# An LSTM of 512 steps on one core: h Wh in 512 columns and one PSUM bank, instead of 384 and 128 columns in two

## The chip, the cores and the metric

The kernel runs on one core of a Trainium2 chip. The metric is the device time of one execution in microseconds (us), lower is better. It is the median of three runs; the trace comes from one further, profiled execution.

## The reference

For 32 sequences (batch B = 32) of T = 512 steps with 512 features, an LSTM with 512 hidden units is run from a given first state, and its outputs are added to the input. Everything is float32.

```python
xW = jnp.einsum('ntd,dg->ntg', x, Wx) + b
def step(carry, xw_t):
    prev_h, prev_c = carry
    a = xw_t + prev_h @ Wh
    i = jax.nn.sigmoid(a[:, :Hd])
    f = jax.nn.sigmoid(a[:, Hd:2 * Hd])
    o = jax.nn.sigmoid(a[:, 2 * Hd:3 * Hd])
    g = jnp.tanh(a[:, 3 * Hd:])
    next_c = f * prev_c + i * g
    next_h = o * jnp.tanh(next_c)
    return ((next_h, next_c), next_h)
...
x = x + hs
```

The part x Wx does not depend on earlier steps. The part h Wh (prev_h @ Wh) and the cell behind it do, so they form a chain through all 512 steps.

## The kernel before

**Layout.** The hidden units are cut into four blocks of 128. A bank of PSUM, `gates[i]` (128 partitions x 512 float32), holds the four gates of one step: partitions 32j to 32j+31 hold the 32 sequences for unit block j, and the 512 columns are the gates i, f, g, o, each with 128 units (`IFG = 3 * P` = 384 is where o begins). There are two such banks. The state h is kept transposed in `ht` (128 x 4 x 32): block k holds units 128k to 128k+127 on the partitions and the 32 sequences in its columns.

**h Wh** (`h_part`, L1051). One matmul has `ht[:, k, :]` as its stationary operand (32 columns) and columns of block (k, j) of Wh as its moving operand; it adds into 32 partitions of a bank. Four matmuls, j = 0 to 3, write four different groups of 32 partitions; below they are called a group. Each float32 matmul is two instructions in the trace, so that one k is two groups. Before the change the gates i, f, g (384 columns) are done for all k first, in the bank `gates[t % 2]`, then o (128 columns) for all k, in the other bank, `gates[(t + 1) % 2]`.

**x Wx** is worked out during the same steps, some 16 steps ahead, by a scheme with fewer multiplications: a block of 8 x 4 rows takes 26 jobs in 32 steps, and a job has seven x products of 256 columns that `IN_STEPS` (L312) spreads over five steps. Such an x product is eight matmul instructions (two groups). After h Wh of a step TensorE therefore has five, six or (early) seven x products to do (`products`, L717). VectorE and ScalarE combine them (`evacuate`, L733: lines 768 to 787, 896, 908, 924), DMAs store the results in DRAM, and further DMAs on the POOL queue add them to a row that ScalarE has filled with the bias (`fill_bias`, L995, `load_xw`, L999).

**The cell** (`cell`, L1082). ScalarE takes sigmoid of i and f (L1092), tanh of g (L1093), sigmoid of o (L1094); VectorE makes f c, i g and their sum c (L1095 to 1097); ScalarE takes tanh of c (L1098); VectorE multiplies by o (L1099) and transposes blocks of 32 x 32 into the next `ht` (L1100). POOL adds the residual (L1162). Then ScalarE puts x Wx of later steps into the banks, as the value to which h Wh is added: `seed_first(k + 2)` the 384 columns of i, f, g (L1040), `seed_last(k + 1)` the 128 of o (L1046).

**Order.** All engines take their instructions in the order of the program text (`manual_schedule`). In step k the main loop (L1410) issues: h Wh of step k; the combining of x products; the x products of this step; loads; the cell of step k; the seeds. So TensorE does h Wh, then x products while ScalarE and VectorE do the cell, then h Wh of the next step, which needs the new `ht`. Semaphores between engines are set by the framework from what the instructions read and write.

**The end.** From step `HALVES` = 472 on, `h_halves` (L1064) and `cell_halves` (L1104) do the cell in two halves of 64 units per block. There the work on the first half is cut further, into pieces of 32 columns (L1132, L1134).

Of the kernel before, what the change touches and what calls it, by code (L numbers as in the profile page):

```python
# [10 lines left out]
AF = mybir.ActivationFunctionType  # L11
# [3 lines left out]
P = 128  # L15
B = 32
T = 512
NJ = 4
G = 4
IFG = 3 * P  # L20
# [145 lines left out]
PAIR_AT = len(UNITS)  # L166
PAIRS = len(PAIR_A_OF)
SECOND_AT = PAIR_AT + PAIRS
OFF = 16
# [22 lines left out]
HALVES = LAST + 3 - OFF  # L192
# [38 lines left out]
LATE_AT = [LAST + 2 + SPACING * u for u in range(NJ + 2)]  # L231
# [6 lines left out]
)  # L238
FILL_FROM, FILL_TO = LAST + 4, T - 4 + OFF
AT_LAST = 3  # L240


class Scheme:
# [68 lines left out]
IN_STEPS = ((4, (4,)), (2, (7,)), (0, (1,)), (1, (6,)), (0, (5,)), (1, (5,)), (3, (2, 3)))  # L312
# [7 lines left out]
def kernel(  # L320
# [9 lines left out]
    nc = tc.nc  # L330
# [11 lines left out]
    gates = [psum.tile([P, G * P], F32, name=f"gates_{i}") for i in range(2)]  # L342
# [14 lines left out]
    rows, xw, stored = {}, {}, {}  # L357
# [109 lines left out]
    late, stored_sums, sums_made = [], set(), []  # L467
# [211 lines left out]
    jobs = {}  # L679
# [283 lines left out]
    pieces = [(t, q, e) for t in range(LATE_END, T - 1) for q in range(NJ) for e in (slice(0, C), slice(C, 2 * C))]  # L963
# [11 lines left out]
    def tail_products(v):  # L975
# [5 lines left out]
        whole.clear()  # L981
        goal = given[1] + (total - 2 * AT_LAST - given[1]) * (v - FILL_FROM) // (FILL_TO - FILL_FROM)
        goal = min(goal, total - 2 * AT_LAST + AT_LAST * max(0, v - FILL_TO))
        while pieces and given[0] < goal:
# [23 lines left out]
    def half(a, m):  # L1008

        return a.rearrange("p (g u) -> p g u", u=P)[:, :, m * HP : (m + 1) * HP]  # L1010

    def bank_half(m, t=0):

        bank = halves[m] if t < T - 1 else jobs[LATE_AT[0]].pp[m].rearrange("p n c -> p (n c)")
        return bank[:, 0 : G * HP].rearrange("p (g u) -> p g u", u=HP)
# [16 lines left out]
    def seed_half(t, m):  # L1032
        if t < T - 1:
            nc.scalar.copy(bank_half(m), half(xw[t], m))

    def seed_first(t):
        if t == HALVES:
            seed_half(t, 0)
        elif t < HALVES:
            nc.scalar.copy(gates[t % 2][:, 0:IFG], xw[t][:, 0:IFG])  # L1040

    def seed_last(t):
        if t == HALVES:
            seed_half(t, 1)
        elif t < HALVES:
            nc.scalar.copy(gates[(t + 1) % 2][:, IFG:], xw[t][:, IFG:])  # L1046

    state.update(c=c_init, ht=h_init)
    ig = work.tile([P, P], F32, name="ig")

    def h_part(t):  # L1051
        for g, cols in ((gates[t % 2], slice(0, IFG)), (gates[(t + 1) % 2], slice(IFG, G * P))):
            for k in range(NJ):
                for j in range(NJ):
                    nc.tensor.matmul(  # L1055
                        g[j * B : (j + 1) * B, cols],
                        state["ht"][:, k, :],
                        wh_sb[:, k, j, cols],
                        start=False,
                        stop=True,  # L1060
                        skip_group_check=True,
                    )
# [19 lines left out]
    def cell(t):  # L1082
        n, tt = divmod(t, ROW)
        s = work.tile([P, G, P], F32, name=f"s_{t}", tag="s")
        fc = work.tile([P, P], F32, name=f"fc_{t}", tag="fc")
        c = work.tile([P, P], F32, name=f"c_{t}", tag="c", bufs=2)
        tc_t, h = ig, fc
        ht = work.tile([P, NJ, B], F32, name=f"ht_{t}", tag="ht", bufs=3)

        g = gates[t % 2].rearrange("p (g u) -> p g u", u=P)  # L1090
        o = gates[(t + 1) % 2].rearrange("p (g u) -> p g u", u=P)[:, 3]
        nc.scalar.activation(s[:, 0:2], g[:, 0:2], AF.Sigmoid)  # L1092
        nc.scalar.activation(s[:, 2], g[:, 2], AF.Tanh)  # L1093
        nc.scalar.activation(s[:, 3], o, AF.Sigmoid)  # L1094
        nc.vector.tensor_mul(fc, s[:, 1], state["c"])  # L1095
        nc.vector.tensor_mul(ig, s[:, 0], s[:, 2])
        nc.vector.tensor_add(c, fc, ig)  # L1097
        nc.scalar.activation(tc_t, c, AF.Tanh)  # L1098
        nc.vector.tensor_mul(h, s[:, 3], tc_t)  # L1099
        nc.vector.transpose(ht.rearrange("p q b -> p (q b)"), h)  # L1100
        state["c"], state["ht"] = c, ht
        put_step(t)

# [68 lines left out]
    for u, (i, j) in zip(UNIT_AT, UNITS):  # L1172
        job = new_job(u)
        job.kind = (i, j)
    for run in RUNS:
        for n in range(run.scheme.r):
            job = new_job(run.at + run.scheme.begin(n), run.scheme.late5(n))
            job.kind = (run, n)
    for w, j in zip(LATE_AT, LATE_ORDER):
        job = new_job(w, True)  # L1180
# [158 lines left out]
    with tc.manual_schedule():  # L1339
        warm = work.tile([P, G, P], F32, name="warm", tag="s")  # L1340
        nc.scalar.activation(warm[:, 0], c_init, AF.Sigmoid)
        zeros = c_init.bitcast(mybir.dt.bfloat16)
        for m in range(16):
            z, times = (zeros, 2) if m < 2 * NJ else (c_init, 4)
            nc.tensor.matmul(
                pps[m // NJ if m < 2 * NJ else 2][m % NJ * B : (m % NJ + 1) * B].rearrange("p n c -> p (n c)"),
                z[:, 0:B],
                z.unsqueeze(1).to_broadcast([P, times, z.shape[1]]),
                start=True,
                stop=True,  # L1350
            )
        made = [prepare(v) for v in range(EARLY)]
        first, second = jobs[0], jobs[1]
        parts = [t_sums(i) for i in (0, NJ)]
        for k in range(2):
            product(first, 1, k)
            product(first, 2, k)
        copy_first(first)
        for op in parts[0]:
            op()  # L1360
        made[0].pop(0)()
        parts[1].pop(0)()
        made[0].pop(0)()
        parts[1].pop(0)()
        product(first, 5)
        copy_fifth(first)
        product(first, 6)
        made[0].pop()()
        product(first, 3)
        product(second, 1)  # L1370
        copy_first(second)
        product(second, 2)
        nc.vector.tensor_add(first.pu[:, 1], first.acc, first.p5)
        parts[1].pop()()
        made[0].pop()()
        for op in (*made[1][:2], made[1][3], made[1][2]):
            op()
        product(second, 5)
        copy_fifth(second)
        product(second, 6)  # L1380
        product(second, 3)
        more = [op for j in range(1, NJ) for op in t_pair(j)]
        more.pop(0)()
        nc.vector.tensor_add(second.pu[:, 1], second.acc, second.p5)
        for v in range(EARLY, OFF):
            head(v)
            if v == NJ + 2:
                nc.vector.transpose(
                    bias_sb.rearrange("p (m l) -> p m l", l=B),
                    bias_t.unsqueeze(2).to_broadcast([P, G * NJ, B]),  # L1390
                )
            if XW_AT <= v + 1 < XW_AT + 4:
                fill_bias(v + 1 - XW_AT)
            announce(v)
            if XW_AT <= v < XW_AT + 3:
                load_xw(v - XW_AT)
            run_due(v + 1, 0)
            evacuate_at_first(v)
            for op in prepare(v):
                op()  # L1400
            for op in more[: NJ + EARLY - v - (v == EARLY)]:
                more.pop(0)()
            run_due(v + 1, (FILL_ROOM if v >= 4 else FILL_ROOM // 2) if v < PAIR_AT else 0)
            products(v)
            fetch(v)
        seed_first(0)
        seed_last(0)
        seed_first(1)

        for k in range(T):  # L1410
            if k % 2 == 0 and k + 2 < T:
                load_residual(k + 2)
            (h_part if k < HALVES else h_halves)(k)
            v = k + OFF
            if v < START + 14:
                head(v)
            announce(v)
            for op in prepare(v):
                op()
            room = HEAD_ROOM if v < START - 4 else ROOM if k < HALVES - 1 else HALF_ROOM  # L1420
            lacks = 0
            if v < START + 8:
                lacks = sum(len(ss) for late, ss in IN_STEPS if v - late not in jobs and (late, ss) != (1, (5,)))
                room -= FEWER * lacks
            run_due(v, room - evacuate(v, room))
            products(v)
            tail_products(v)
            if k + 3 < LATE_END:
                load_xw(k + 3)
            store_sums()  # L1430
            fetch(v)
            if k == T - 2:
                x_last()
            if k + 4 < LATE_END and lacks < 2:
                fill_bias(k + 4)
            (cell if k < HALVES else cell_halves)(k)
            if k + 4 < LATE_END and lacks >= 2:
                fill_bias(k + 4)
            seed_first(k + 2)
            seed_last(k + 1)  # L1440
        assert not due


# [49 lines left out]
```

## Time and profile before

| | |
|---|---|
| median of 3 runs | 3069.54 us (3068.2 to 3071.56) |
| profiled execution, first to last instruction (span) | 3067.7 us; no other time of this execution is given |
| granted TensorE clock | 1.000 |
| VectorE busy | 2322.4 us (76%) |
| ScalarE busy | 2001.6 us (65%) |
| POOL busy | 832.4 us (27%) |

In the rows below, PE is TensorE's matmuls, PEld its weight loads, DVE VectorE, ACT ScalarE. A row of the timeline has the start and the duration in us, the engine, the line, the operation, the tile written and the tiles read, the shapes, the count of instructions that were merged, and in brackets the idle time of the engine before it and what ended it. A row of groups has the busy time in us and the mean duration in ns behind the first bar, and the idle time before the group behind the second. The ends of matmuls are modelled, so starts are used.

### The profile page before, as it was taken

The page shows a single profiled execution, that of the slowest core. Times are in us where ns is not written, and L with a number is a line of the kernel's source. Part 1 is how long each engine was busy: PE and PEld are TensorE (multiplying, and loading weights), DVE is VectorE, ACT ScalarE, POOL GpSimd, SP SyncE. Part 2 cuts the span into 40 slices and gives each one's busy share as a digit, 9 for nine tenths or more (in the row PEclk, how much of TensorE's full clock was granted, in tenths as well). Part 3 has the DMA queues.
Part 4 walks back from the last instruction along what each step waited for, and adds up shares of the span by engine and source line. Part 5 has one row for each costly group of instructions (what it writes and reads, how often), then busy time and mean ns, then how long its engine had stood idle before and what let it go on. Part 6 is the DMA issues. An engine that isn't in the chain of part 4 may idle for free.

```text
span 3067.7 us, 133937 instructions
## 1 busy us (share of the span) xinstructions
PE 3059.4 (100%) x56568; PEld 2303.0 (75%) x56568; DVE 2322.4 (76%) x6622; ACT 2001.6 (65%) x5774; POOL 832.4 (27%) x1041
## 2 busy tenths in 40 slices
PE   9999999999999999999999999999999999999999
PEld 5566666667777777777777777777777777777766
DVE  7888777777777777777777777777777777777754
ACT  4666666666666666666666666766666666666665
POOL 0233222222222222222222222222222222222331
PEclk9999999999999999999999999999999999999999
DMA  9999898988889888898888988889898898888763
GB/s 330 291 272 266 230 253 213 255 232 234 245 212 260 227 237 246 215 262 215 257 227 214 271 218 244 233 222 261 216 253 232 222 259 222 250 233 220 199 120 72
DMA packets 345192, 716.21 MB, mean 233 GB/s; under 512 B 45712, under 2 KB 112016, under 8 KB 344080
## 3 DMA queue, kind: packets, MB, share of 16 engines
q1 hardware_dynamic: 268768, 564.74, 56.0%
q0 software_dynamic: 75392, 142.38, 27.9%
q8 instruction: 445, 7.29, 1.0%
q14 instruction: 155, 1.27, 0.1%
q10 hardware_dynamic: 432, 0.53, 0.1%
HBM read 521.48 MB, written 185.99 MB: 231 GB/s over the span
## 4 chain that ended last, share of the span: by engine, by line
PE 99%; DVE 0%; ACT 0%; DMA 0%; issue 0%; SPq 0%; ACTq 0%; DVEq 0%
PE gates L1055 52%; PE pp L708 18%; PE acc L708 18%; PE p L708 6%; PE gates L1069 4%; PE acc L950 0%; DMA raw_sb<-in_L_cond_Wx_dram 0%; PE pp L1069 0%; PE pp L950 0%; PE gates L708 0%; PE pp L1023 0%; DVE fc L1132 0%; ACT s L1114 0%; DVE ht L1134 0%; DVE c L1122 0%
## 5 line engine op out<-in xcount | busy, mean ns | idle before, releaser
L1055 PE MATMUL gates<-wh_sb,ht 128*32 128x384 f32 (+1 forms) x30144 | 1771.8, 379 | 0.4 <-ACT tt_sb L896 0.3
L1055 PEld LDWEIGHTS gates<-wh_sb,ht 128*32 128x32 f32 x30144 | 1318.1, 110 | 431.7 <-issue 131.1
L1162 POOL TENSOR_TENSOR oc<-xr,ht 128x128 f32<-128x128 f32 x509 | 389.2, 765 | 2108.0 <-DVE ht L1100 1919.5
L1001 POOL DMA_DIRECT2D xw<-xw x508 | 446.7, 879 | 93.3 <-DVE s L667 62.2
L1092 ACT ACTIVATE s<-gates 128x256 f32<-128x256 f32 x472 | 181.2, 384 | 350.5 <-PE gates L1055 340.2
L708 PE MATMUL pp<-wb,nodes 128*32 128x256 f32 x4000 | 370.9, 379 | 0.0
L997 ACT COPY xw<-bias_sb 128x512 f32<-128x512 f32 x508 | 320.9, 632 | 0.0
L776 ACT COPY pp<-pu 128x512 f32<-128x512 f32 x404 | 243.4, 602 | 57.4 <-DVE raw_sb L908 23.9
L1099 DVE TENSOR_TENSOR fc<-s,ig 128x128 f32<-128x128 f32 x472 | 137.9, 292 | 177.4 <-ACT ig L1098 177.4
L1095 DVE TENSOR_TENSOR fc<-s,c 128x128 f32<-128x128 f32 x471 | 136.7, 290 | 169.0 <-ACT s L1092 165.8
L708 PE MATMUL pp<-wb,s 128*32 128x256 f32 x2704 | 250.4, 379 | 0.0
L708 PE MATMUL acc<-wb,s 128*32 128x256 f32 x2704 | 250.3, 379 | 0.0
L708 PE MATMUL acc<-wa,s 128*32 128x256 f32 x2704 | 250.1, 379 | 0.0
L708 PE MATMUL p<-wa,s 128*32 128x256 f32 x2704 | 249.9, 379 | 0.0
L778 DVE TENSOR_TENSOR pp<-acc,p 128x256 f32<-128x256 f32 x406 | 173.4, 427 | 99.7 <-ACT pp L777 99.2
L1094 ACT ACTIVATE s<-gates 128x128 f32<-128x128 f32 x472 | 130.8, 277 | 147.5 <-PE gates L1055 147.4
L1040 ACT COPY gates<-xw 128x384 f32<-128x384 f32 x472 | 223.2, 473 | 0.2
L1098 ACT ACTIVATE ig<-c 128x128 f32<-128x128 f32 x472 | 146.3, 310 | 101.8 <-DVE c L1097 64.6
L777 ACT COPY pp<-acc 128x256 f32<-128x256 f32 x406 | 146.7, 361 | 98.6 <-DVE raw_sb L908 36.6
L708 PEld LDWEIGHTS pp<-wb,nodes 128*32 128x32 f32 x4000 | 186.8, 110 | 26.1
L768 DVE TENSOR_TENSOR pu<-acc,p 128x256 f32<-128x256 f32 x404 | 167.8, 415 | 43.2 <-ACT p L787 34.8
L708 PE MATMUL acc<-wa,nodes 128*32 128x256 f32 x2000 | 185.0, 379 | 0.0
(317 smaller groups left out, 4758.7 us busy)
## 6 DMA issues: line engine op xcount, KB each, us to landing
wb<-keep_b SPq DMA_DIRECT2D x338, 512.0 KB, 6.2
xw<-xw POOLq DMA_DIRECT2D x508, 256.0 KB, 5.6
wa<-keep_a SPq DMA_DIRECT2D x338, 384.0 KB, 5.2
xw<-raw_sb SPq DMA_DIRECT2D x408, 128.0 KB, 3.6
xw<-tt_sb SPq DMA_DIRECT2D x332, 128.0 KB, 3.9
xr<-in_x_dram SPq DMA_DIRECT2D x256, 128.0 KB, 5.5
out_dram<-oc SPq DMA_DIRECT2D x255, 128.0 KB, 4.3
row<-in_x_dram SPq DMA_DIRECT2D x63, 512.0 KB, 8.2
```

Of the source, the lines that this page charges most:

```text
L708: nc.tensor.matmul(dst[t * B : (t + 1) * B], a[:, t % a.shape[1]], w[t // a.shape[1]] if isinstance(w, list) else w, start=(s in (1, 5) or ...
L768: nc.vector.tensor_add(job.pu[:, 1], job.acc, job.p5)
L776: nc.scalar.copy(job.pp[0], job.pu)
L777: nc.scalar.copy(job.pp[1][:, 0], job.acc)
L778: nc.vector.tensor_add(job.pp[1][:, 1], job.acc, job.p5)
L997: nc.scalar.copy(xw[t], bias_sb)
L1001: nc.gpsimd.dma_start(out=xw[t], in_=stored[i][a], accum_op=mybir.AluOpType.add)
L1040: nc.scalar.copy(gates[t % 2][:, 0:IFG], xw[t][:, 0:IFG])
L1055: nc.tensor.matmul(g[j * B : (j + 1) * B, cols], state["ht"][:, k, :], wh_sb[:, k, j, cols], start=False, stop=True, skip_group_check=True,)
L1092: nc.scalar.activation(s[:, 0:2], g[:, 0:2], AF.Sigmoid)
L1098: nc.scalar.activation(tc_t, c, AF.Tanh)
L1162: (nc.gpsimd if t < T - 3 else nc.vector).tensor_add(state["oc"][:, tt % 2], xr[t][:, tt % 2], ht)
```

## The change

- For the steps t = 1 to 470 (those before `HALVES` with at least five x products behind them, `in_one`), all four gates of step t are in one bank, `gates[t % 2]`.
- Where six or seven x products follow (325 of these steps), h Wh is sixteen matmuls of 512 columns, k by k.
- Where five follow (145 steps), the first two row blocks (k = 0, 1) are in 512 columns; the other two are done in 384 columns and then in 128 columns, in the same bank.
- The seeds of a step that follows another such step are one copy of 512 columns instead of two of 384 and 128.
- In the cell of these steps, tanh of c, the product with o and the transpose are each cut in two, 32 columns and 96 columns; the order is both tanh, both products, both transposes. The first transpose gives block k = 0 of the next `ht`.

```diff
+WHOLE_FROM = 6
...
+    def filling(v):
+        found = 0
+        for late, ss in IN_STEPS:
+            job = jobs.get(v - late)
+            if job and job.w < LATE_AT[0]:
+                found += sum((1 if job.w >= PAIR_AT else 2) for s in ss if s != 5 or job.w5 == v)
+        return found
+
+    def in_one(t):
+
+        return 0 < t < HALVES and filling(t + OFF) >= 5
+
+    def out_bank(t):
+        return gates[t % 2 if in_one(t) else (t + 1) % 2]
+
     def seed_first(t):
...
-            nc.scalar.copy(gates[t % 2][:, 0:IFG], xw[t][:, 0:IFG])
+            end = G * P if in_one(t) and in_one(t - 1) else IFG
+            nc.scalar.copy(gates[t % 2][:, 0:end], xw[t][:, 0:end])
 
     def seed_last(t):
...
-        elif t < HALVES:
-            nc.scalar.copy(gates[(t + 1) % 2][:, IFG:], xw[t][:, IFG:])
+        elif t < HALVES and not (in_one(t) and in_one(t - 1)):
+            nc.scalar.copy(out_bank(t)[:, IFG:], xw[t][:, IFG:])
+
+    def seed_next(k):
+        seeds = [lambda: seed_first(k + 2), lambda: seed_last(k + 1)]
+        for seed in reversed(seeds) if in_one(k + 1) else seeds:
+            seed()
...
     def h_part(t):
-        for g, cols in ((gates[t % 2], slice(0, IFG)), (gates[(t + 1) % 2], slice(IFG, G * P))):
-            for k in range(NJ):
+        if not in_one(t):
+            parts = ((gates[t % 2], slice(0, IFG), (0, 1, 2, 3)), (gates[(t + 1) % 2], slice(IFG, G * P), (0, 1, 2, 3)))
+        elif filling(t + OFF) >= WHOLE_FROM:
+            parts = ((gates[t % 2], slice(0, G * P), (0, 1, 2, 3)),)
+        else:
+            parts = tuple(
+                (gates[t % 2], slice(a, b), ks)
+                for a, b, ks in ((0, G * P, (0, 1)), (0, IFG, (2, 3)), (IFG, G * P, (2, 3)))
+            )
+        for g, cols, ks in parts:
+            for k in ks:
...
-        o = gates[(t + 1) % 2].rearrange("p (g u) -> p g u", u=P)[:, 3]
+        o = out_bank(t).rearrange("p (g u) -> p g u", u=P)[:, 3]
...
-        nc.scalar.activation(tc_t, c, AF.Tanh)
-        nc.vector.tensor_mul(h, s[:, 3], tc_t)
-        nc.vector.transpose(ht.rearrange("p q b -> p (q b)"), h)
+        pieces = [slice(a * B, b * B) for a, b in (((0, 1), (1, NJ)) if in_one(t) else ((0, NJ),))]
+        for u in pieces:
+            nc.scalar.activation(tc_t[:, u], c[:, u], AF.Tanh)
+        for u in pieces:
+            nc.vector.tensor_mul(h[:, u], s[:, 3, u], tc_t[:, u])
+        for u in pieces:
+            nc.vector.transpose(ht.rearrange("p q b -> p (q b)")[:, u], h[:, u])
...
-            seed_first(k + 2)
-            seed_last(k + 1)
+            seed_next(k)
```

## The prediction, made before the result was known

> **What bounds the kernel now.** I read the page first: the busy shares and the chain that ended last.
>
> ```profile
> span 3067.7 us, 133937 instructions
> PE 3059.4 (100%) x56568; PEld 2303.0 (75%) x56568; DVE 2322.4 (76%) x6622; ACT 2001.6 (65%) x5774; POOL 832.4 (27%) x1041
> ...
> PE 99%; DVE 0%; ACT 0%; DMA 0%; issue 0%; SPq 0%; ACTq 0%; DVEq 0%
> PE gates L1055 52%; PE pp L708 18%; PE acc L708 18%; PE p L708 6%; PE gates L1069 4%; PE acc L950 0%; DMA raw_sb<-in_L_cond_Wx_dram 0%; PE pp L1069 0%; PE pp L950 0%; PE gates L708 0%; PE pp L1023 0%; DVE fc L1132 0%; ACT s L1114 0%; DVE ht L1134 0%; DVE c L1122 0%
> ```
>
> TensorE is never idle. Time can be saved only by shortening its stream, and any wait that appears in it is paid in full. So the question is twofold: how much shorter is the stream, and does the next h still arrive before TensorE wants it? For this I took a step with five x products from the timeline (the rows of one cell, and TensorE's).
>
> ```profile
> 1116.13 3.68 PE L1055 MATMUL gates<-wh_sb,ht 128*32 128x384 f32 x61
> ...
> 1119.10 0.38 ACT L1092 ACTIVATE s<-gates 128x256 f32<-128x256 f32 x1 [0.93 <-PE gates L1055]
> ...
> 1119.52 0.29 DVE L1095 TENSOR_TENSOR fc<-s,c 128x128 f32<-128x128 f32 x1 [0.51 <-ACT s L1092]
> ...
> 1119.58 0.38 PE L708 MATMUL pp<-wb,nodes 128*32 128x256 f32 x1
> ...
> 1119.73 0.28 DVE L1096 TENSOR_TENSOR ig<-s 128x128 f32<-128x128 f32 x1
> ...
> 1119.98 0.28 ACT L1094 ACTIVATE s<-gates 128x128 f32<-128x128 f32 x1 [0.32 <-PE gates L1055]
> ...
> 1120.37 0.31 ACT L1098 ACTIVATE ig<-c 128x128 f32<-128x128 f32 x1
> ...
> 1121.11 0.31 DVE L1100 STREAM_TRANSPOSE ht<-fc 128x128 f32<-128x128 f32 x1
> ...
> 1121.74 0.66 PE L1055 MATMUL gates<-wh_sb,ht 128*32 128x384 f32 x4
> ```
>
> The step lasts 1121.74 - 1116.13 = 5.61 us: 3.45 of h Wh up to the first x product at 1119.58, then five x products of 2.16 / 5 = 0.432. The sigmoid of o starts 0.40 after o's last group was issued (1119.98 - 1119.58). The same 0.40 before 1119.10 puts the end of i, f, g at 1118.70, so o takes 0.88. From the first sigmoid to tanh of c is 1.27, from there to the transpose 0.74.
>
> How long TensorE takes from the transpose to its first matmul is seen only where it had to wait, as in this earlier step:
>
> ```profile
> 305.44 0.31 DVE L1100 STREAM_TRANSPOSE ht<-fc 128x128 f32<-128x128 f32 x1
> ...
> 305.90 0.53 PE L1055 MATMUL gates<-wh_sb,ht 128*32 128x384 f32 x4
> ```
>
> 0.46 from start to start, 0.15 of it behind the transpose's end. So the cell **needs** 0.40 + 1.27 + 0.74 + 0.46 = 2.87 after the last group of i, f, g. TensorE's **cover** for it is o and the x products: 0.88 + 2.16 = 3.04 in a step with five, 3.47 with six. Slack: 0.17 and 0.60. Every step is covered, the five-product ones barely.
>
> **What is saved.** A group is four matmuls side by side. By the rows above a group of 256 columns costs 0.216 (half an x product), one of 128 columns 0.109 to 0.110 (0.88 / 8; other steps show 0.87). If each is a fixed part f plus a part for its columns, f = 2 x 0.109 - 0.216, about 0.0025 with a spread from 0.0015 to 0.004. A pair of 384 and 128 columns becomes one group of 512: it saves one f. A step with six or seven x products has eight such pairs (saves 0.02), one with five has four (saves 0.01). The jobs' places in the code give 22 steps with six and 10 with five x products in each block of 32 (26 jobs x 7 = 182 = 22 x 6 + 10 x 5). Over steps 1 to 470 that is 314 with six, 11 with seven, 145 with five. Saved: 325 x 0.02 + 145 x 0.01 = **8 us** (5 to 13). The first and the last steps, and the 40 in halves, stay.
>
> **What is moved: o's cover.** In a whole step all gates end together, so ScalarE's first sigmoid can start only 0.40 after the end of h Wh, and o's 0.88 no longer covers anything: the cover is 2.59 with six, 2.16 with five, 3.02 with seven x products.
>
> For the steps with five, the text writes o last, so that i, f and g end 4 x 0.11 = 0.44 earlier. But o now goes to the bank that the sigmoid of i and f reads. Whether that read waits for o's matmuls depends on how the semaphores are set: by columns or by bank. The trace of before has one clear case. L777 (ScalarE) and L778 (VectorE) write different halves of one bank, both read `acc`, and neither reads what the other writes.
>
> ```profile
> L778 DVE TENSOR_TENSOR pp<-acc,p 128x256 f32<-128x256 f32 x406 | 173.4, 427 | 99.7 <-ACT pp L777 99.2
> ```
>
> Of 99.7 us that VectorE idled before L778, 99.2 ended with L777. Accesses to one bank are ordered whatever their columns. So I take it that L1092 waits for all of o, and that the split of k = 2, 3 buys nothing: the cover is 2.16.
>
> The Trainium skill has a rule for this: "PSUM — Partial Sum Buffer", section "PSUM bank collisions raise a hardware error", says that two engines on one bank and the same 32 partitions at one time raise an error even at different columns, and that one should guard PSUM by bank and quadrant rather than by address. The trace agrees as far as the 99.2 us above; by this rule the sum is the one below, and with reads ordered by columns it would be that of the second rival.
>
> **What is added: the cut cell.** Tanh, product and transpose in 32 and 96 columns let the matmuls of k = 0 start earlier. Before does something like it at its end, in halves:
>
> ```profile
> 2952.95 0.26 ACT L1139 ACTIVATE ig<-c 128x64 f32<-128x64 f32 x1
> 2953.12 0.26 ACT L1114 ACTIVATE s<-gates 128x128 f32<-128x128 f32 x1
> 2953.24 0.29 DVE L1132 TENSOR_TENSOR fc<-s,ig 128x32 f32<-128x32 f32 x2 [0.32 <-ACT ig L1139]
> ...
> 2953.54 0.30 DVE L1134 STREAM_TRANSPOSE ht<-fc 128x32 f32<-128x32 f32 x2
> ...
> 2953.90 3.66 PE L1069 MATMUL gates<-wh_sb,ht 128*32 128x256 f32 x64 [0.24 <-DVE ht L1134]
> ```
>
> From tanh to the waiting matmul 0.95, with a tanh of 64 columns, products of 32 and 32, transposes of 32 and 32; uncut it was 0.74 + 0.46 = 1.20. The change's own sequence:
>
> ```profile
> L1098 ACT ACTIVATE ig<-c 128x128 f32<-128x128 f32 x472 | 146.3, 310 | 101.8 <-DVE c L1097 64.6
> ...
> L1134 DVE STREAM_TRANSPOSE ht<-fc 128x32 f32<-128x32 f32 x78 | 12.0, 192 | 1.1 <-DVE fc L1132 0.4 <-DVE ht L1134 0.2
> ...
> L1132 DVE TENSOR_TENSOR fc<-s,ig 128x32 f32<-128x32 f32 x78 | 11.5, 189 | 12.6 <-ACT ig L1139 12.6
> ...
> L1139 ACT ACTIVATE ig<-c 128x64 f32<-128x64 f32 x40 | 10.2, 256 | 2.8 <-DVE c L1122 1.1
> ```
>
> On the line through 310 ns (128 columns) and 256 (64), a tanh of 32 columns takes 0.23 and one of 96 0.28. The second starts 0.14 after the first (the row behind L1139 starts 0.17 later, 0.09 less than its 0.26) and ends at 0.42. The second product starts 0.03 later, at 0.45, and since VectorE takes its queue in order, the first transpose starts behind it, 0.17 later (between 0.21 for 128 columns, L1095 to L1096, and 0.10 for 32), at 0.62. With 0.20 for itself and 0.15 to the matmul: **0.97**. Ends: 0.90 (quicker than the halves' 0.95 by the smaller tanh, and a little more) and 1.05 (another 0.08 for the wait on the longer product). The second transpose is done about 0.15 after TensorE has started on k = 0, whose two groups last 0.86, so k = 1 does not wait for it.
>
> The new need is 0.40 + 1.27 + 0.97 = 2.64 behind the end of h Wh. Behind TensorE's wait for the first transpose stands its whole queue, so each stall is paid:
>
> - five x products: 2.64 - 2.16 = 0.48, x 145 = 69.6 us
> - six: 2.64 - 2.59 = 0.05, x 314 = 15.7 us
> - seven: none
>
> **Costed at nothing.** ScalarE's seeds become one copy (512 columns instead of 384 and 128); ScalarE idles 0.93 before L1092 above, and without that cover the copy would add nothing either, being shorter than the two. POOL's sum and the DMAs behind it wait for the second transpose, off the path. VectorE and ScalarE get their combining work later against h Wh, by up to 0.9 us in a step with six:
>
> ```profile
> 1005.86 1.22 DVE L924 TENSOR_TENSOR raw_sb<-raw_sb 128x1024 f32<-128x1024 f32 x1
> 1006.44 0.38 ACT L1092 ACTIVATE s<-gates 128x256 f32<-128x256 f32 x1 [0.41 <-PE gates L1055]
> ...
> 1007.00 0.28 DVE L1095 TENSOR_TENSOR fc<-s,c 128x128 f32<-128x128 f32 x1
> ...
> 1010.79 0.42 DVE L768 TENSOR_TENSOR pu<-acc,p 128x256 f32<-128x256 f32 x1 [0.79 <-ACT p L787]
> ```
>
> Here L924 holds back the first product (0.56 behind L1092 instead of 0.42 in the other step). In before the slack hides that. Afterwards L1092 itself comes 0.88 later against h Wh, which is more than L924 reaches, and idle stretches like the 0.79 take up the later start. If that cover fails, an average 0.1 in steps with six adds 31 us; this widens the upper end.
>
> **The sum.** Against the profiled execution's span: 69.6 + 15.7 - 8 = +77. Its 3067.7 lies 1.8 below the median of the runs, 3069.5, which includes what lies around the span; I add to the median: **3147 us**. With 0.90 for the cut cell: 0.41 x 145 + 0 - 8 = +51, 3121; with 1.05: 0.56 x 145 + 0.13 x 314 - 8 = +114, 3184.
>
> **Rivals.**
> 1. *VectorE stays late* in steps with six: 3147 + 31 = 3178. For it: the L924 row; against it: the idle rows.
> 2. *Semaphores by columns*: in steps with five L1092 starts 0.44 earlier, stall 0.04: 145 x 0.04 + 15.7 - 8 = +13.5, 3083 us. For it: the split of k = 2, 3 gives steps with five a cover of 0.44 + 2.16 = 2.60, just that of six; against it: the L778 row.
> 3. *Faster*: as the second, and the first piece is ready 0.05 sooner because its transpose needn't queue behind the 96-column product. It decides from a need of 2.59 down; then nothing stalls and the 8 us stay: 3061 us. For it: the halves' 0.95 with a longer tanh.
> 4. *The cut buys nothing*, TensorE waiting for both transposes (the change then not doing what it says): 1.20 again, stalls of 0.71 and 0.28: +183, 3252 us. Against it: in the row of 2953.90 TensorE started 0.06 after the end of both transposes, 0.15 after the end of the first.
>
> **Chances.** Forecast 0.80; rival one 0.07; two 0.06; three 0.04; four 0.03. The range 3117 to 3184 takes in the ends of the cut cell and rival one, and leaves out the other three (0.13) and a few hundredths of the forecast. Measurements of this kernel tell about 0.2% (6 us) from no change. Faster than that: rival three and a bit for its edge, 0.05; within: 0.05, from the lower edge of rival two; slower: 0.90.
>
> **What would show it.** Right: in the profile after, idle time of TensorE of some 85 us ended by the transpose (about 0.48 in steps with five, 0.05 with six), steps of about 6.08 us in both kinds, L1092 0.40 behind the *last* of the 128-column groups. Wrong: L1092 in steps with five starting while o's matmuls are still running; no idle time before L1055 in steps with six; or a 512-column group far from 0.429.

## The result, and the profile after

The changed kernel takes 3110.9 us in the median (3110.4 at the lowest); its ratio to the kernel before is 1.0134, with a 95% interval from 1.0121 to 1.0148. That is 41.5 us slower. One of the change's four runs, at a granted clock of 0.843, took 3592.4 us and is not in the ratio. The forecast was 77 slower, with a range that began at 3117: the sign was right, the size was not.

The page after, first the span, the busy times, then the chain that ended last, then one group:

```profile
span 3108.6 us, 109516 instructions
...
PE 3082.7 (99%) x43848; PEld 1410.7 (45%) x43848; DVE 2387.3 (77%) x7562; ACT 1895.1 (61%) x5775; POOL 823.1 (26%) x1041
...
PE 87%; DVE 7%; ACT 3%; issue 2%; DMA 1%; SPq 0%; POOL 0%; ACTq 0%; DVEq 0%; POOLq 0%
...
L1123 ACT ACTIVATE s<-gates 128x256 f32<-128x256 f32 x472 | 181.4, 384 | 627.1 <-PE gates L1086 627.0
```

Busy time hides the loss: TensorE still reads 99%, because the ends of matmuls are modelled. The chain shows it. Before, 99% of it ran on TensorE; now 13% of it runs elsewhere, 10% through VectorE and ScalarE, by way of the cell. ScalarE's first sigmoid (L1123, before L1092) now waits 627 us for h Wh; before, it was

```profile
L1092 ACT ACTIVATE s<-gates 128x256 f32<-128x256 f32 x472 | 181.2, 384 | 350.5 <-PE gates L1055 340.2
```

How a single step looks, from the timeline after (a step with six x products from 1088.68, one with five from 1094.70, one with six from 1100.59; L1086 is h Wh, L709 an x product, L1131 tanh of c, L1135 the transposes):

```profile
1088.68 3.62 PE L1086 MATMUL gates<-wh_sb,ht 128*32 128x512 f32 x32
...
1094.27 0.61 PE L709 MATMUL pp<-wb,s 128*32 128x256 f32 x8
1094.30 0.40 DVE L1135 STREAM_TRANSPOSE ht<-fc 128x32 f32<-128x32 f32 x2
...
1094.56 0.27 PEld L1086 LDWEIGHTS gates<-wh_sb,ht 128*32 128x32 f32 x8 [0.16 <-DVE ht L1135]
...
1094.70 3.63 PE L1086 MATMUL gates<-wh_sb,ht 128*32 128x512 f32 x48
...
1098.14 0.61 PE L709 MATMUL pp<-wb,nodes 128*32 128x256 f32 x8
...
1098.39 0.38 ACT L1123 ACTIVATE s<-gates 128x256 f32<-128x256 f32 x1 [2.73 <-PE gates L1086]
...
1099.72 0.40 ACT L1131 ACTIVATE ig<-c 128x32 f32<-128x32 f32 x2 [0.61 <-DVE c L1128]
1099.87 0.61 PE L709 MATMUL p<-wa,s 128*32 128x256 f32 x8
...
1100.33 0.40 DVE L1135 STREAM_TRANSPOSE ht<-fc 128x32 f32<-128x32 f32 x2
...
1100.59 0.16 PEld L1086 LDWEIGHTS gates<-wh_sb,ht 128*32 128x32 f32 x8 [0.59 <-DVE ht L1135]
1100.59 3.64 PE L1086 MATMUL gates<-wh_sb,ht 128*32 128x512 f32 x32
...
1106.64 3.62 PE L1086 MATMUL gates<-wh_sb,ht 128*32 128x512 f32 x32
```

In the step with six, the transposes start at 1094.30, the first weights are loaded at 1094.56, and the matmul follows the last x product without a gap (1094.27 + 0.43 = 1094.70). In the step with five the last x product starts at 1099.87 and would end at 1100.30; the transposes only start at 1100.33, and h Wh begins at 1100.59. TensorE stands still for **0.29**. The need behind the end of h Wh is 1100.59 - 1098.14 = 2.45.

The same reading, done for every step from the start of its first h Wh matmul to that of the next (less 3.43 to 3.45 for h Wh, a little different in each kernel, and 0.4316 for each x product), gives the waits of TensorE that the tables below call "stalls". Before: 1.5 us in all. After: 47.3 in the 145 steps with five x products (0.29 to 0.32 in 137 of them, 0.23 in one, 0.48 to 1.94 in seven) and 3.5 in those with six. The balance closes: 47.3 + 3.5 - 1.5 us more of waits, 8.0 less for matmuls (h Wh takes 3.434 instead of 3.454 in steps with six, 3.444 in those with five), so +41.3, against +40.9 between the spans.

### The profile page after: what moved, and what is told of

The parts are those of the page before. It is cut to its first block, busy times and chain, and to the rows that moved or that the text cites. A ratio compares the mean times of both kernels' runs of the same rounds, so it can differ in the third digit from the quotient of the medians.

```text
span 3108.6 us, 109516 instructions
## 1 busy us (share of the span) xinstructions
PE 3082.7 (99%) x43848; PEld 1410.7 (45%) x43848; DVE 2387.3 (77%) x7562; ACT 1895.1 (61%) x5775; POOL 823.1 (26%) x1041
## 4 chain that ended last, share of the span: by engine, by line
PE 87%; DVE 7%; ACT 3%; issue 2%; DMA 1%; SPq 0%; POOL 0%; ACTq 0%; DVEq 0%; POOLq 0%
PE gates L1086 52%; PE pp L709 14%; PE acc L709 11%; PE p L709 4%; PE gates L1100 4%; ACT s L1123 2%; DVE c L1128 1%; DVE fc L1126 1%; DVE fc L1133 1%; ACT ig L1131 1%; DVE ht L1135 1%; DVE ig L1127 1%; DMA keep_b<-scratch 0%; DMA keep_a<-scratch 0%; PE acc L951 0%
## 5 line engine op out<-in xcount | busy, mean ns | idle before, releaser
L1086 PE MATMUL gates<-wh_sb,ht 128*32 128x512 f32 (+2 forms) x17424 | 1708.8, 536 | 18.6 <-DVE ht L1135 3.7
L1086 PEld LDWEIGHTS gates<-wh_sb,ht 128*32 128x32 f32 x17424 | 541.9, 110 | 1019.5 <-issue 817.7
L1123 ACT ACTIVATE s<-gates 128x256 f32<-128x256 f32 x472 | 181.4, 384 | 627.1 <-PE gates L1086 627.0
L1131 ACT ACTIVATE ig<-c 128x32 f32<-128x32 f32 (+2 forms) x942 | 189.9, 248 | 280.9 <-DVE c L1128 280.6
L1133 DVE TENSOR_TENSOR fc<-s,ig 128x32 f32<-128x32 f32 (+2 forms) x942 | 203.3, 226 | 159.7 <-ACT ig L1131 159.7
L709 PE MATMUL pp<-wb,nodes 128*32 128x256 f32 x4000 | 307.4, 379 | 0.0
L1057 ACT COPY gates<-xw 128x512 f32<-128x512 f32 (+1 forms) x472 | 272.3, 577 | 0.0
L709 PE MATMUL acc<-wb,s 128*32 128x256 f32 x2704 | 207.9, 379 | 0.1
L709 PE MATMUL acc<-wa,s 128*32 128x256 f32 x2704 | 207.9, 379 | 0.0
L709 PE MATMUL pp<-wb,s 128*32 128x256 f32 x2704 | 207.8, 379 | 0.0
L709 PE MATMUL p<-wa,s 128*32 128x256 f32 x2704 | 207.8, 379 | 0.0
L779 DVE TENSOR_TENSOR pp<-acc,p 128x256 f32<-128x256 f32 x406 | 173.1, 426 | 42.4 <-ACT pp L778 41.6
L709 PEld LDWEIGHTS pp<-wb,nodes 128*32 128x32 f32 x4000 | 128.5, 110 | 147.8 <-issue 74.2
L1135 DVE STREAM_TRANSPOSE ht<-fc 128x32 f32<-128x32 f32 (+2 forms) x942 | 187.0, 236 | 2.3 <-DVE fc L1133 1.8
L769 DVE TENSOR_TENSOR pu<-acc,p 128x256 f32<-128x256 f32 x404 | 167.0, 413 | 18.2 <-ACT p L788 8.6
L784 ACT COPY pu<-acc 128x256 f32<-128x256 f32 x406 | 150.2, 370 | 19.9 <-DVE pp L779 13.7
```

The lines of the kernel that those rows point to most:

```text
L709: nc.tensor.matmul(dst[t * B : (t + 1) * B], a[:, t % a.shape[1]], w[t // a.shape[1]] if isinstance(w, list) else w, start=(s in (1, 5) or ...
L779: nc.vector.tensor_add(job.pp[1][:, 1], job.acc, job.p5)
L1057: nc.scalar.copy(gates[t % 2][:, 0:end], xw[t][:, 0:end])
L1086: nc.tensor.matmul(g[j * B : (j + 1) * B, cols], state["ht"][:, k, :], wh_sb[:, k, j, cols], start=False, stop=True, skip_group_check=True,)
L1131: nc.scalar.activation(tc_t[:, u], c[:, u], AF.Tanh)
L1133: nc.vector.tensor_mul(h[:, u], s[:, 3, u], tc_t[:, u])
```

## The experiments

Eleven more kernels ran. Times are medians, ratios are to the kernel before (run again beside each group of them) with their 95% intervals, stalls are sums in us over the steps with five and with six or seven x products.

| kernel | us | ratio | stalls five / six, seven |
|---|---|---|---|
| before | 3069.4 | 1 | 0.4 / 1.2 |
| the change | 3110.9 | 1.0134 [1.0121, 1.0148] | 47.3 / 3.5 |
| e3: o of k = 2, 3 to the other bank | 3065.9 | 0.9991 [0.9982, 1.0000] | 3.8 / 1.8 |
| e2: steps with five whole too | 3109.0 | 1.0128 [1.0112, 1.0143] | 46.4 / 4.3 |
| e1: steps with five as before | 3070.3 | 1.0004 [0.9995, 1.0012] | 5.4 / 4.1 |
| e4: the change, cell uncut | 3153.5 | 1.0275 [1.0261, 1.0289] | 72.5 / 20.5 |
| e6: before, o's groups first | 3204.1 | 1.0437 [1.0423, 1.0452] | 85.7 / 49.3 |
| e8: before, cell cut | 3069.2 | 1.0000 [0.9991, 1.0009] | 0.5 / 0.7 |
| e5: the change, seeds in two copies | 3115.6 | 1.0149 [1.0133, 1.0164] | 53.9 / 1.5 |
| e7: e1 with the cut in all steps | 3067.0 | 0.9990 [0.9981, 0.9999] | 3.1 / 2.8 |
| e9: the change, cell cut from f c on | 3074.8 | 1.0016 [1.0007, 1.0025] | 7.2 / 8.8 |
| e10: e9, steps with five whole | 3070.5 | 1.0005 [0.9996, 1.0014] | 5.9 / 5.9 |
| e11: e10, early cut in steps with five alone | 3070.3 | 1.0003 [0.9994, 1.0012] | 5.8 / 6.5 |

### Does the sigmoid of i, f wait for o, because they share a bank? (e3, e2)

e3 sends o of k = 2, 3 to the other bank, in steps with five; half of o's h Wh is thereby missing from these steps, and nothing in the order of the instructions changes.

```diff
-                (gates[t % 2], slice(a, b), ks)
-                for a, b, ks in ((0, G * P, (0, 1)), (0, IFG, (2, 3)), (IFG, G * P, (2, 3)))
+                (gates[(t + far) % 2], slice(a, b), ks)
+                for a, b, ks, far in ((0, G * P, (0, 1), 0), (0, IFG, (2, 3), 0), (IFG, G * P, (2, 3), 1))
```

> In steps with five the last eight groups (o of k = 2, 3, 128 columns) add to the o columns of the other bank, so that half of h Wh of o is missing in these steps and is added to the next step's o; widths, counts and order of the matmuls are those of the changed kernel. Theory (order by bank): the sigmoid of i and f starts 0.44 earlier against the end of h Wh, the cover of 2.16 becomes 2.60, over the need of 2.45, the waits of these steps go, 3064 us (3060 to 3070). Rival (order by columns, or the wait has another cause): 3111 us as before.

Timeline of e3, one step with five:

```profile
1118.72 0.38 ACT L1123 ACTIVATE s<-gates 128x256 f32<-128x256 f32 x1 [1.48 <-PE gates L1086]
...
1118.91 0.61 PE L709 MATMUL pp<-wb,nodes 128*32 128x256 f32 x8
...
1120.66 0.40 DVE L1135 STREAM_TRANSPOSE ht<-fc 128x32 f32<-128x32 f32 x2
...
1121.07 3.63 PE L1086 MATMUL gates<-wh_sb,ht 128*32 128x512 f32 x48
```

The sigmoid starts 0.19 *before* the end of h Wh (1118.91); in the change it started 0.25 behind it. The difference is 0.44, o's four groups. h Wh follows the last x product at once (1118.91 + 2.16 = 1121.07), and 45 us are gone. So in the change L1123 waits for o's 128-column groups only because they are in its bank; columns don't come into it. The rule of the Trainium skill that the prediction weighed ("PSUM — Partial Sum Buffer", section "PSUM bank collisions raise a hardware error": guard by bank, not by address) agrees with that 0.44.

The other side of the same thing is e2: if the split of k = 2, 3 buys nothing, leaving it out costs nothing.

```diff
-WHOLE_FROM = 6
+WHOLE_FROM = 5
```

> Steps with five take 512 columns for all four row blocks, like those with six. Theory (the sigmoid of i and f waits for everything in its bank, so the split of k = 2, 3 buys nothing): the wait stays as it is, about 0.31 a step, and 145 x 0.01 are saved, 3109.5 us (3107 to 3112). Rival (the read is ordered by columns, so the split lets it start 0.44 earlier): 145 x 0.44 more, 3175 us.

It took 3109.0. A step with five stalls 0.29 to 0.32 as in the change, and the 1.9 us are about what four more pairs of groups save in 145 steps (1.5).

### Are the steps with five all of the loss? (e1)

```diff
-        return 0 < t < HALVES and filling(t + OFF) >= 5
+        return 0 < t < HALVES and filling(t + OFF) >= WHOLE_FROM
```

> Steps with five x products keep the two banks and the uncut cell of the kernel before; steps with six or seven are as in the changed kernel. Theory (the whole loss is TensorE waiting for the transpose in the 145 steps with five): no wait of that kind is left and 325 x 0.02 = 6.5 us are saved, 3063 us (3060 to 3067). Rival (one bank and the cut cell cost something in every step): a steady loss stays in the steps with six, over 3075 us.

The 41 us are gone, so they are all of it. But the 6.5 us that 325 whole steps save do not show: 3070.3, a miss. The trace has 9.5 us of stalls instead of 1.5. Some are long and early; one of about 0.17 comes back every 32 steps, here:

```profile
676.79 0.68 DVE L909 TENSOR_TENSOR slot_h<-pp,slot_h 128x512 f32<-128x512 f32 x1
677.01 0.39 ACT L1123 ACTIVATE s<-gates 128x256 f32<-128x256 f32 x1 [1.24 <-PE gates L1086]
...
677.92 0.28 DVE L1126 TENSOR_TENSOR fc<-s,c 128x128 f32<-128x128 f32 x1
...
679.96 0.53 PE L1086 MATMUL gates<-wh_sb,ht 128*32 128x384 f32 x4
```

VectorE makes f c 0.91 behind the sigmoid instead of 0.42 because its combining (L909 and what follows it) lies in front, and the uncut cell has no room for that in a step with five (e7, below, cuts it, and 14 such waits become two).

### What the cut is worth, and what o's cover was worth (e4, e6, e8)

e4 is the change without the cut:

```diff
-        pieces = [slice(a * B, b * B) for a, b in (((0, 1), (1, NJ)) if in_one(t) else ((0, NJ),))]
+        pieces = [slice(a * B, b * B) for a, b in ((0, NJ),)]
```

> The changed kernel with tanh, product and transpose of the cell uncut. Theory (the need behind the end of h Wh is 2.45 with the cut cell; uncut the transpose ends 0.24 later): 0.24 more in each step with five and a wait of about 0.1 in each with six: 145 x 0.24 + 314 x 0.1 = 66, 3177 us (3150 to 3185). Rival (TensorE waits for both transposes anyway, the cut buys nothing): 3111 us.

It took 3153.5, inside the range but 24 us below the figure expected. The need is 2.62 (h Wh's end, 1112.32, to the next h Wh, 1114.94), so the cut gives 0.17 in a step, not 0.24, and 43 us in all. The other 0.06 or so lies ahead of tanh, which starts 0.55 behind ScalarE's last work in e4 and 0.61 behind it in the change; e5 below comes back to this.

```profile
1112.32 0.61 PE L709 MATMUL pp<-wb,nodes 128*32 128x256 f32 x8
...
1113.84 0.31 ACT L1131 ACTIVATE ig<-c 128x128 f32<-128x128 f32 x1 [0.55 <-DVE c L1128]
...
1114.58 0.31 DVE L1135 STREAM_TRANSPOSE ht<-fc 128x128 f32<-128x128 f32 x1
...
1114.94 3.64 PE L1086 MATMUL gates<-wh_sb,ht 128*32 128x512 f32 x32 [0.28 <-DVE ht L1135]
```

e6 has nothing of the change in it; it only moves o's groups ahead of those of i, f, g, so that o no longer lies between the end of i, f, g and the next h:

```diff
-        for g, cols in ((gates[t % 2], slice(0, IFG)), (gates[(t + 1) % 2], slice(IFG, G * P))):
+        for g, cols in ((gates[(t + 1) % 2], slice(IFG, G * P)), (gates[t % 2], slice(0, IFG))):
```

> The kernel before with one edit: the 128-column groups of o come ahead of the 384-column groups of i, f, g, in two banks as before, and the cell uncut. Nothing of the change's 512 columns or cut is in it; only o's 0.88 us no longer lies between the end of i, f, g and the next h. Theory: that cover alone is the loss. Need behind the end of h Wh, uncut: 0.25 + 1.27 + 0.74 + 0.31 (transpose) + 0.05 to 0.15 = 2.62 to 2.72; stalls of 0.46 to 0.56 in 145 steps with five x products and 0.03 to 0.13 in 314 with six: 67 to 81 plus 9 to 41, so 3146 to 3192 us. Rival: the bank or the 512 columns of the change cost the time, not the lost cover: 3069 us (below 3085).

3204.1: the rival falls, and the loss is even 12 us above the theory's upper end. A step with five stalls 0.575, one with six 0.145; the need is 2.74, of which 0.147 lie between the transpose's end and the matmul. A few early steps, with longer waits, add some 4 us.

So the loss comes in a ladder, each rung of it a run: o's cover taken away costs 135 us (3069 to 3204); 512 columns and one seed copy give back 51 (3204 to 3153), 42 of them waits and 8 matmul time; the cut gives back 43 more (3153 to 3111). Where nothing waits, the cut alone gives nothing. e8 is the kernel before with

```diff
-        nc.scalar.activation(tc_t, c, AF.Tanh)
-        nc.vector.tensor_mul(h, s[:, 3], tc_t)
-        nc.vector.transpose(ht.rearrange("p q b -> p (q b)"), h)
+        pieces = [slice(a * B, b * B) for a, b in ((0, 1), (1, NJ))]
+        for u in pieces:
+            nc.scalar.activation(tc_t[:, u], c[:, u], AF.Tanh)
+        for u in pieces:
+            nc.vector.tensor_mul(h[:, u], s[:, 3, u], tc_t[:, u])
+        for u in pieces:
+            nc.vector.transpose(ht.rearrange("p q b -> p (q b)")[:, u], h[:, u])
```

> The kernel before with the cut cell alone, in steps in which every cell is covered. Theory: the cut is worth something only where TensorE waits; here it does not, so 3069 us, within 2 us (before's own 1.5 us of waits may go). Rival: three more instructions a step on ScalarE and VectorE push the combining work back until TensorE waits for it: over 3075.

3069.2 it is, the ratio 1.0000.

### What the need is made of (e5)

In e5 the seed of o is always a copy of its own behind the cell:

```diff
-            end = G * P if in_one(t) and in_one(t - 1) else IFG
+            end = IFG
...
-        elif t < HALVES and not (in_one(t) and in_one(t - 1)):
+        elif t < HALVES:
```

> The changed kernel, but ScalarE's seed is always two copies (i, f, g one step ahead, o behind the cell), so that the first matmul of h Wh again waits for two semaphores, VectorE's transpose and a ScalarE copy. Theory: the second semaphore is what made the way from the transpose to the first matmul 0.147 us in the kernel before and 0.054 in the changed one; with it back the need grows by 0.093, to 2.54, so a step with five x products stalls 0.38 instead of 0.29: 145 x 0.093 = 13.5 us more, 3124 us (3119 to 3130); a step with six (cover 2.59) still does not stall. Rival: the 0.147 was the misaligned column tiles of the kernel before, not the semaphore; then no change, 3111 us (below 3114).

Its time of 3115.6 lies between the two figures expected, and inside neither range. By the lines' own views, which count every kind of instruction of a line (PEldq is the sequencer of the weight loads; first before, then the change, then e5):

```profile
L1055 PEldq EVENT_SEMAPHORE  x472: 51/51/51, 73.3 to 2863.7; - x158
```
```profile
L1086 PEldq EVENT_SEMAPHORE  x2: 51/51/51, 73.4 to 79.2; - x2
```
```profile
L1086 PEldq EVENT_SEMAPHORE  x471: 51/51/51, 73.6 to 2904.4; - x157
```

Before, each step's first weight load needed a separate instruction of 51 ns to wait for a second semaphore (ScalarE's seed of o, beside VectorE's transpose). With one seed copy, a step ahead, it is gone; e5 brings it back:

```profile
1133.25 0.40 ACT L1131 ACTIVATE ig<-c 128x32 f32<-128x32 f32 x2 [0.55 <-DVE c L1128]
...
1133.56 0.26 ACT L1063 COPY gates<-xw 128x128 f32<-128x128 f32 x1
...
1133.86 0.40 DVE L1135 STREAM_TRANSPOSE ht<-fc 128x32 f32<-128x32 f32 x2
1134.18 0.19 PEld L1086 LDWEIGHTS gates<-wh_sb,ht 128*32 128x32 f32 x8 [0.32 <-ACT gates L1063]
...
1134.21 3.65 PE L1086 MATMUL gates<-wh_sb,ht 128*32 128x512 f32 x48
```

From the end of the first transpose (0.205 behind 1133.86) to the matmul it is 0.146, in the change 0.054: the theory's 0.092 is there, and the rival falls. The releaser named is the seed (L1063), but it had ended 0.25 before the transpose did. What the theory left out is in the first row. In e5 tanh starts 0.55 behind ScalarE's last work, in the change 0.61: there tanh has semaphore instructions of its own (319 on L1131, in e4 and e5 none), so that e5 gains 0.06 back. The need is 2.50, 0.05 more than in the change and not 0.09 (the sigmoid, 0.27 instead of 0.25 behind h Wh, gives the rest). Why the change needs these instructions on tanh was not settled.

### Can the 8 us be had? (e7, e9, e10, e11)

e7 is e1 with the cut cell in all steps before `HALVES`:

```diff
-        pieces = [slice(a * B, b * B) for a, b in (((0, 1), (1, NJ)) if in_one(t) else ((0, NJ),))]
+        pieces = [slice(a * B, b * B) for a, b in (((0, 1), (1, NJ)) if t < HALVES else ((0, NJ),))]
```

> Steps with five x products in the old form (384 and 128 columns, two banks), steps with six or seven in 512 columns, and the cut cell in all of them, where the run with the old form in steps with five had it only in steps with 512 columns. Theory: what that run (3070.3) gave back of the 6.5 us saved were short waits where VectorE came late to the cell, about 0.1 us each; the cut takes 0.17 off the need of the steps with five, so most of them vanish: 3066 us (3063 to 3069). Rival: the waits come from elsewhere, and it stays at 3070.

3067.0 is inside the range expected and 2.3 us below the kernel before, 0.1% with an interval from 0.01% to 0.19%: it is the only kernel with all of the work that beats both, and barely. Of the 14 waits of about 0.17 in e1 two are left (0.12 and 0.16), as the theory had it; ten of 0.41 to 0.58 in steps with five remain, and their cause was not followed.

e9 takes the change and cuts the whole cell from the product f c on; here `u` is the first 32 columns and `w` the other 96:

```diff
+        for v in (u, w) if w else (u,):
+            nc.vector.tensor_mul(fc[:, v], s[:, 1, v], state["c"][:, v])
+            nc.vector.tensor_mul(ig[:, v], s[:, 0, v], s[:, 2, v])
+            if v is u:
+                nc.vector.tensor_add(c[:, u], fc[:, u], ig[:, u])
+                nc.scalar.activation(tc_t[:, u], c[:, u], AF.Tanh)
+        nc.vector.tensor_mul(h[:, u], s[:, 3, u], tc_t[:, u])
+        if w:
+            nc.vector.tensor_add(c[:, w], fc[:, w], ig[:, w])
+            nc.scalar.activation(tc_t[:, w], c[:, w], AF.Tanh)
+        nc.vector.transpose(flat[:, u], h[:, u])
...
```

> The changed kernel with the cell cut earlier: the products with f and i, the sum c, tanh, the last product and the transpose are each done for 32 columns first and then for 96, instead of the last three alone. Theory: the chain behind the end of h Wh is all that TensorE waits for; the first transpose then starts at about 1.85 (0.85 for the tanh of g, 0.22 to the sum, 0.25 to tanh, 0.26 to the product, 0.27 for the sum of the 96 columns put between) instead of 2.19, so the need is 2.11 instead of 2.45, under the cover of 2.16: the stalls of 47 us in steps with five x products go, 3064 us (3061 to 3070). Rival: six more instructions in the cell keep VectorE, 77% busy, from its combining work, and TensorE waits for that instead: over 3080.

e10 is e9 with `WHOLE_FROM = 5`, as in e2.

> The same with steps of five x products whole too: all eight pairs of groups in 512 columns instead of four. Theory: with the stalls gone the second half of the pairs saves another 0.01 in 145 steps, 1.5 us below the run with the earlier cut alone: about 3062 us (3059 to 3069). Rival: no difference between the two, or this one slower by the steps' o coming with i, f, g.

The chain came out as worked out: the transpose starts 1.84 behind the end of h Wh (1132.07 to 1133.91) and TensorE does not wait in this step with five (1132.07 + 2.16 = 1134.23):

```profile
1132.07 0.61 PE L709 MATMUL acc<-tt_sb,s 128*32 128x256 f32 x8
...
1132.32 0.38 ACT L1123 ACTIVATE s<-gates 128x256 f32<-128x256 f32 x1 [0.77 <-PE gates L1086]
...
1133.91 0.21 DVE L1138 STREAM_TRANSPOSE ht<-fc 128x32 f32<-128x32 f32 x1
...
1134.22 3.62 PE L1086 MATMUL gates<-wh_sb,ht 128*32 128x512 f32 x32
```

The 47 us went, but the time did not come down to 3064: e9 took 3074.8 and e10 3070.5, both outside the ranges expected. Between the two lie 4.3 us instead of 1.5, because e9 waits longer in its first steps (7.8 us in the first 36, against 3.0). TensorE now waits for something else. The waits of the weight loads for the accumulator's bank (engine, tile and line, releaser: sum, times, longest; about 0.3 of each is no loss), first the change, then e10:

```profile
PEld acc L709 <- DVE pu L769: 4.7, 16, 0.3
...
PEld acc L709 <- DVE pp L779: 1.1, 4, 0.3
```
```profile
PEld acc L709 <- DVE pp L779: 32.7, 92, 1.2
...
PEld acc L709 <- DVE pu L769: 20.3, 45, 0.7
```

VectorE, 83% busy in e10 instead of 77%, reads the accumulator (L779, L769) too late for the next x product. I took its load for the cause and gave the early cut to the steps with five alone, in e11:

```diff
+        if in_one(t) and filling(t + OFF) < 6:
...
+        else:
...
+            pieces = [slice(a * B, b * B) for a, b in (((0, 1), (1, NJ)) if in_one(t) else ((0, NJ),))]
...
```

> 512 columns in all steps with five or more x products, as in the last run, but the early cut (from the product with f on) only in the steps with five, which need it; steps with six or seven keep the change's cut from tanh on, whose need of 2.40 to 2.45 is under their cover of 2.59. Theory: the 11.8 us of waits left in the last run come from VectorE's three additional instructions a step, which make its combining late (TensorE waits for the accumulator's bank, L779 and L769); without them in 325 of 470 steps about half of these waits go: 3064 us (3059 to 3068), the 9.4 us saved by 512 columns showing at last. Rival: the waits hang on the steps with five alone, and it stays at 3070.

That theory fell. VectorE is down to 79%, and the time stays at 3070.3, as the rival had it. The waits stand at fixed places of the 32-step pattern: two come back in each block (0.30 and 0.23), both in a step behind one with five. This is the second in e11, and below it the start of the same step in the kernel before, which does not wait:

```profile
708.08 3.62 PE L1086 MATMUL gates<-wh_sb,ht 128*32 128x512 f32 x32
...
708.67 1.18 DVE L925 TENSOR_TENSOR slot_h<-slot_h,tt_sb 128x1024 f32<-128x1024 f32 x1
...
711.95 0.61 PE L709 MATMUL acc<-wa,row 128*32 128x256 f32 x8
...
712.11 0.42 DVE L779 TENSOR_TENSOR pp<-acc,p 128x256 f32<-128x256 f32 x1
...
712.59 0.16 PEld L709 LDWEIGHTS acc<-wa,s 128*32 128x32 f32 x8 [0.51 <-DVE pp L779]
712.59 0.64 PE L709 MATMUL acc<-wa,s 128*32 128x256 f32 x8
```
```profile
707.38 1.18 DVE L924 TENSOR_TENSOR slot_h<-slot_h,tt_sb 128x1024 f32<-128x1024 f32 x1
...
707.77 3.68 PE L1055 MATMUL gates<-wh_sb,ht 128*32 128x384 f32 x61
```

The third x product should start at 712.38 and waits for L779's end at 712.53. The combining in front of L779 is one run without a gap, and it begins (L925, L924 in before) when the cell of the step before is done. In e11 that is 0.59 after h Wh has begun (708.67 - 708.08), in before 0.39 ahead of it: without o's cover the cell lies 0.98 later against the matmuls, and the combining behind it moves with it. Moving that combining in the order by hand was not tried.

## Why the prediction was right in kind and wrong in size

- **The saving, 8 us: right.** h Wh is 0.020 shorter in steps with six or seven x products and 0.010 in those with five.
- **Which engine, and which wait: right.** The loss is TensorE waiting for the transpose in steps with five; o's cover was what hid it (e6).
- **Order by bank: right** (e3, e2). The second rival, semaphores by columns, falls: e3 is what it would have looked like.
- **The need, 2.64: wrong; it is 2.45.** This is the step that failed, in three terms:
  - *Sigmoid, 0.40 behind the end of h Wh: it is 0.25.* The row that gave 0.40 (1119.58) had a count of one: one of the x product's eight matmuls ran ahead of the other seven. In the kernel before, the four column groups (the four matmuls of a group, each on its own 32 partitions) are not in step; in 369 of its steps the first is 0.16 ahead, so most other steps would have given 0.40 too. In the timeline of before, one step ahead of a wait, and the step after it:

```profile
303.49 0.38 PE L708 MATMUL acc<-wb,s 128*32 128x256 f32 x1
...
303.58 0.29 PE L1055 MATMUL gates<-wh_sb,ht 128*32 128x128 f32 x3
303.69 0.61 PE L708 MATMUL acc<-wb,s 128*32 128x256 f32 x7
...
303.92 0.28 ACT L1094 ACTIVATE s<-gates 128x128 f32<-128x128 f32 x1 [0.32 <-PE gates L1055]
...
309.35 0.64 PE L708 MATMUL pp<-wb,nodes 128*32 128x256 f32 x8
...
309.61 0.28 ACT L1094 ACTIVATE s<-gates 128x128 f32<-128x128 f32 x1 [0.32 <-PE gates L1055]
```

  At 303.49 one matmul of the x product starts while three of h Wh are still to come at 303.58; the sigmoid is 0.43 behind the first and 0.23 behind the other seven. At 305.90 TensorE waited (the prediction quotes that row), and a step later all eight stand in one row, with the sigmoid 0.26 behind. In the change the four are within about 0.02 in every step. Its waits bring them together, but e9 has them together as well in the step without a wait shown above; what lets the first run ahead in the kernel before was not settled.
  - *From the transpose's end to the matmul, 0.15: it is 0.054.* The 0.15 came from a load with two semaphores; one seed copy made it one (e5). The prediction looked at the seeds for ScalarE's time alone and costed them at nothing; they gained 0.09 in each stalled step.
  - *From the first sigmoid to tanh, 1.27: it is 1.33*, by a second semaphore on tanh. The cut cell up to the transpose was right: 0.61 for 0.62.
- **The sum.** With 2.45 the forecast's own arithmetic gives 145 x 0.29 = 42, nothing in steps with six, less 8: +34, 3104. No wait in steps with six was one of the prediction's own signs of being wrong, and it came. The rest to 3111 is mainly 0.024 of restart in each step behind a stall, some 4 us, and seven single long waits, some 3 us more than 0.29 each, whose cause I did not follow (the longest, 1.9 us, is in the first 32 steps). That the sign came out right is no luck, since the loss stands where the prediction put it; 70 of its 85 us of waits were put on steps with five, and these lost 47.
- **The range** took the ends of the cut cell alone. The other two terms were given no ends, though the 0.40 rested on one step and the 0.15 on another.
- **VectorE's lateness, costed at nothing:** right for the change (3.5 us in steps with six or seven); wrong as a general step. In e1, e9, e10 and e11 it takes back a part of what they save, by the waits shown above; their longer, early waits were not followed.
- **The other rivals.** *The cut buys nothing* falls by e4 (43 us). *Faster* asked for a need of 2.59 at most and for order by columns; the first came, the second did not. *VectorE stays late* in steps with six did not show in the change (3.5 us in all).

## What to carry to other kernels

Before two results are put into one instruction or one bank, ask who waits for the earlier of them: here 8 us of matmuls were saved, and 0.88 us of a step that had hidden the way to the next h were given away. Take a latency from a step in which the engine really waited, and look at the counts of the rows: a "x1" beside a "x7" means that the start belongs to the quickest and not to the result. When a wait on the longest chain is removed, run the kernel with the trace once more, since the next limit (here VectorE's release of an accumulator) was only 0.1 to 0.3 us behind it.

## What the runs showed of the hardware

- The four column groups of a matmul group are not always in step: in before the first runs up to 0.2 us ahead of the others (303.49 against 303.69), and the wait at 305.90 brings them together. In the change they are in step throughout.
- In these kernels a second semaphore on a weight load costs 0.09 us between the releaser's end and the matmul (0.146 in e5 against 0.054 in the change), more than the 51 ns of its own instruction.
- A step that starts behind a wait is 0.024 us longer (6.047 against 6.023 in steps with six; in the stretch above 1100.59 to 1106.64 against 1088.68 to 1094.70), even though nothing in it waits again: its first group of matmuls lasts 0.453 instead of 0.430 (from 1100.593 and from 1094.699, before rounding). In e5, where the first load has two semaphores, it is not (6.023).
- Float32 matmuls of 128, 256, 384 and 512 columns, four side by side, take 0.109, 0.216, 0.322 and 0.429 us: a fixed part of about 0.0025 us (the 0.020 that eight merges save in a step, by eight), so there was little to save here by wider ones.
